# A diagonal LSTM and a quantum convolution on one core: the order of work inside the scan's ramp steps

## The chip, the core and the metric

The kernel runs on one core of a Trainium2 chip. The metric is the device time of one execution in microseconds, smaller is better. The core has five engines that run side by side, each working through its own queue in order: PE multiplies matrices (PEld is its loading of the weights, which can overlap a running product), DVE and ACT do element-wise work, POOL does element-wise work too and issues DMAs, SP issues DMAs. An engine waits for another by a semaphore.

## The reference

The input x has 16 images, 128 channels and 64 x 64 pixels. Layer 0 adds to x a diagonal LSTM of the group-normalised x; layer 1 adds a 1x1 quantum convolution of the result's group norm. The change touches layer 0 only:

```python
xs = skew(x)                                   # row i shifted right by i
i_s = einsum('oi,bihw->bohw', w_is, xs) + b_is
def step(carry, ist):
    h, c = carry
    h_shift = pad(h, ((0, 0), (0, 0), (1, 0)))[:, :, :-1]   # the row above
    s_s = einsum('oi,bih->boh', w_ss[:, :, 0], h_shift) + einsum('oi,bih->boh', w_ss[:, :, 1], h) + b_ss[None, :, None]
    gates = ist + s_s
    ofi = sigmoid(gates[:, :3 * C])
    o, f, ig = ofi[:, :C], ofi[:, C:2 * C], ofi[:, 2 * C:]
    g = tanh(gates[:, 3 * C:])
    c_new = f * c + ig * g
    h_new = o * tanh(c_new)
    return (h_new, c_new), h_new
_, hs = lax.scan(step, (h0, c0), i_s_t)
x = x + unskew(moveaxis(hs, 0, 3), W)
# layer 1: x + post_w @ simulate(pre_w @ group_norm(x))
```

A step of the scan works on one anti-diagonal. A row that the skewed picture has not reached sees zero input, so its state is the same for all images until its first pixel comes.

## The kernel before

It runs in three stages: the first group norm's statistics while x is loaded; the scan; then the second group norm and layer 1, which read and write DRAM. The work inside the scan is written under a manual schedule, so each engine's order is the order of the lines.

**Tiling of the scan.** Channels lie on the 128 partitions. The 64 rows are taken as two bands of 32 slots; band 1 starts BAND = 65 steps after band 0, and a slot that band 0 has left is taken by the row of band 1, so there are NSTEP = 160 steps, t = 0 to 159. Even slots are half q = 0 and odd slots half q = 1 of every tile, [128, 2, 256]; a column is one image of one slot, 16 (NB) to a slot. `columns(t)` gives the active columns a to b: they widen from 16 to 256 in steps 0 to 31, stay at 256 up to step 129, and shrink afterwards. `reach(t)` adds four columns past b, in which one column carries the state of the row that still waits for its first pixel.

**Two kinds of step.** A step whose half is at most FEW = 96 columns wide (`plain(t)`: steps 0 to 11 and 148 to 159) multiplies both halves of h by w1T and, shifted by a row, by w0T, for each gate (L768 to L771). The other 136 steps use that the row above an odd slot is the even slot of the same column: they multiply the even half of h by wsT = w0T + w1T into half 0 of all four gates (L774 to L775), ACT copies that half out (L789 to L792), and then each gate gets w1T times the difference of the two halves of h in half 1 and w0T times the difference towards the slot above in half 0 (L795 to L798). DVE adds the copy to half 1 (`add`, L757 to L760). `differences` (L602 to L610) makes the first difference on DVE (L604), the second on POOL (L607, L610). The gates go in the order ORDER = GF, GI, GG, GO (forget, input, candidate, output).

**The end of a step.** ACT applies the gate functions (`activate`, L762 to L766); DVE multiplies c by F (L806), then I by G (L812), adds it to c by halves (L815), ACT takes the tanh by halves (L816), and DVE multiplies by O into the next h by halves (L825). `gate_ps(t + 1)` (L578 to L593) puts the input products of the next step (L585) on PE meanwhile.

**New rows.** When a slot becomes active, `begin` (L599 to L600) spreads its one-column state over the 16 images: h from hinv on DVE, c from cinv on ACT (L829 to L831), in every step t with t + 1 < 32 for band 0, and with 64 <= t <= 95 for band 1. `waits` (L713 to L734) makes the next waiting state: its inner function `state` (L720 to L721) multiplies one column on DVE, once or twice, and POOL copies it into hinv and cinv.

**POOL and DVE beside it.** POOL subtracts the mean and scales by rstd for step t + 2 (`normalised`, L557 to L576), adds h to x in the ring (`residual`, L612 to L619), and keeps the last slot of band 0 as the edge for band 1 (L842 to L843). DVE takes the second norm's statistics as rows are finished (`statistics`). Four more operations on POOL prepare for the second norm: three memsets and one scaling, L642 to L645, which stand ahead of the scan.

Of the kernel before, what the change touches and what calls it, by code (L numbers as in the profile page):

```python
# [11 lines left out]
F32 = mybir.dt.float32  # L12
# [4 lines left out]
P = 128  # L17
NB = 16
NH = 64
NW = 64  # L20
SLOTS = 32
PAIRS = SLOTS // 2
NC = PAIRS * NB
RING = 40
ROWS = 4
BLOCK = ROWS * NW
# [2 lines left out]
FIRST = 8  # L29
LATE = 4  # L30
FEW = 96
LEAST = 128
AHEAD = RING - SLOTS
BAND = NW + 1
# [6 lines left out]
GO, GF, GI, GG = 0, 1, 2, 3  # L41
FUNC = {GO: AF.Sigmoid, GF: AF.Sigmoid, GI: AF.Sigmoid, GG: AF.Tanh}
ORDER = (GF, GI, GG, GO)
# [37 lines left out]
def kernel(  # L81
# [16 lines left out]
    nc = tc.nc  # L98
# [16 lines left out]
    group = wide_sb[:, 0:128]  # L115
# [7 lines left out]
    NG2 = NH // 4  # L123
# [32 lines left out]
    with ExitStack() as scan:  # L156
# [4 lines left out]
        wsT = wpool.tile([P, 512], F32, name="wsT")  # L161
        bias = wpool.tile([P, 4], F32, name="bias")

        hinv = wpool.tile([P, NH], F32, name="hinv")
        cinv = wpool.tile([P, NH], F32, name="cinv")
        state = scan.enter_context(tc.tile_pool(name="state", bufs=1))
# [50 lines left out]
        with ExitStack() as prep:  # L217
# [139 lines left out]
            for i in range(2):  # L357
                v = ws_n[i]
# [64 lines left out]
            ps = ps_small.tile([P, NB], F32, name="gv1", tag="small")  # L423
# [75 lines left out]
        work = scan.enter_context(tc.tile_pool(name="work", bufs=1))  # L499
        cst = work.tile([P, 2, NC], F32, name="cst")  # L500
# [10 lines left out]
        def columns(t):  # L511
            lo, hi = active(t)
            return lo // 2 * NB, (hi + 1) // 2 * NB
# [6 lines left out]
        def plain(t):  # L520
            a, b = columns(t)
            return b - a <= FEW

        def wide(t, least=LEAST):

            a, b = columns(t)[0], reach(t)
            return max(0, min(a, b - least)), max(b, min(NC, a + least))
# [50 lines left out]
        def gate_ps(t):  # L578

            a, b = wide(t, LEAST // 2)  # L580
            ps = {} if t else first
# [17 lines left out]
        def begin(copy, v, s, of, r):  # L599
            copy(one_slot(v, s), of[:, r : r + 1].to_broadcast([P, NB]))  # L600
# [37 lines left out]
        added = work.tile([P, 2, NB, 2], F32, name="added")  # L638
        inner = work.tile([P, NB, 2], F32, name="inner")
        sums_of = work.tile([P, 2, 2, NB], F32, name="sums_of")  # L640
        by_one = work.tile([P, P], F32, name="by_one")
        for v in (added, inner, sums_of):  # L642
            nc.gpsimd.memset(v, 0.0)
        by_half = group
        nc.gpsimd.tensor_scalar_mul(by_one, group, 1.0 / (NG2 * BLOCK))  # L645

        def early_sums():
            k = 2 * FIRST
# [64 lines left out]
        def waits(t, v, th, o, new):  # L713


            j = EARLY + t + 1
            to = columns(t + 1)[1]
            q = 1 if plain(t) else 0

            def state(at):  # L720
                nc.vector.tensor_mul(at, th[:, q, v : v + 1], o[:, q, v : v + 1])  # L721

            if to < NC:
                for k in range(q + 1):
                    if k != q or to > v:
                        state(new[:, k, to : to + 1])
                nc.gpsimd.tensor_copy(hinv[:, j : j + 1], new[:, q, to : to + 1])
            else:
                state(hinv[:, j : j + 1])
            nc.gpsimd.tensor_copy(cinv[:, j : j + 1], cst[:, q, v : v + 1])  # L730
            if to < NC:
                q1 = 1 if plain(t + 1) else 0
                if to > v or q1 != q:
                    nc.gpsimd.tensor_copy(cst[:, q1, to : to + 1], cinv[:, j : j + 1])  # L734

        def step(t, ps):

            a, b = columns(t)
            few = plain(t)
            a0, b0 = wide(t, LEAST // 2 if few else LEAST)  # L740
            w = reach(t)
            now, new, diff = hst[t % 2], hst[(t + 1) % 2], dst[t % 2]

            def product(g, out, w, rhs):
                nc.tensor.matmul(  # L745
                    out,
                    lhsT=w[:, g * 128 : (g + 1) * 128],
                    rhs=rhs,
                    start=False,
                    stop=True,  # L750
                    skip_group_check=True,
                )

            def half(g, q, w, rhs):
                product(g, ps[g][:, q, a0:b0], w, rhs[:, a0:b0])

            def add(g):  # L757
                if g in both:
                    v = ps[g][:, 1, a:b]
                    nc.vector.tensor_add(v, v, both[g][:, a:b])  # L760

            def activate(g):  # L762
                to = act[GG] if g == GG else ps[g]
                nc.scalar.activation(  # L764
                    to[:, :, a:w], ps[g][:, :, a:w], FUNC[g], bias=bias[:, g : g + 1]
                )  # L766

            if few and t:  # L768
                for g in ORDER:
                    product(g, ps[g][:, :, a0:b0], w1T, now[:, :, a0:b0])  # L770
                    product(g, ps[g][:, :, a0:b0], w0T, above(now, a0, b0))  # L771
            elif t:
                differences(t, now, diff)
                for g in ORDER:  # L774
                    half(g, 0, wsT, now[:, 0])  # L775
            if t > SLOTS:
                for _ in range(3):
                    next(steps, None)
            ready, sums[:] = list(sums), []
            statistics(4 if w - a <= LEAST else 6)  # L780
            if t:
                residual(t - 1, now)
            if t + 2 < NSTEP:
                normalised(t + 2)
            for later in ready:
                if next(later, True) is None:
                    sums.append(later)
            both = {}
            if not few:  # L789
                for g in ORDER:  # L790
                    both[g] = work.tile([P, NC], F32, name=f"both{t}_{g}", tag=f"both{g}")
                    nc.scalar.copy(both[g][:, a:b], ps[g][:, 0, a:b])  # L792
            act = {g: ps[g] for g in ORDER}
            act[GG] = work.tile([P, 2, NC], F32, name=f"g{t}", tag="g")
            if not few:  # L795
                for g in ORDER:
                    half(g, 1, w1T, diff[:, 1])
                    half(g, 0, w0T, diff[:, 0])  # L798
            add(GF)
            activate(GF)  # L800
            add(GI)
            activate(GI)
            add(GG)
            activate(GG)
            c = cst[:, :, a:w]
            nc.vector.tensor_mul(c, c, act[GF][:, :, a:w])  # L806
            add(GO)
            activate(GO)
            later = gate_ps(t + 1) if t + 1 < NSTEP else None

            ig = act[GI][:, :, a:w]
            nc.vector.tensor_mul(ig, ig, act[GG][:, :, a:w])  # L812
            th = act[GG]
            for q in range(2):
                nc.vector.tensor_add(c[:, q], c[:, q], ig[:, q])  # L815
                nc.scalar.activation(th[:, q, a:w], c[:, q], AF.Tanh)  # L816
            fresh = [
                (s, SLOTS * band + s)
                for band in range(2)
                for s in [t + 1 - BAND * band]  # L820
                if 0 <= s < SLOTS
            ]
            for q in range(2):
                v = w if q == few and columns(t + 1)[1] == b else b
                nc.vector.tensor_mul(new[:, q, a:v], th[:, q, a:v], act[GO][:, q, a:v])  # L825
                if q == few and w > b:
                    waits(t, b, th, act[GO], new)
                for s, r in fresh:
                    if s % 2 == q:  # L829
                        begin(nc.vector.tensor_copy, new, s, hinv, r)  # L830
                        begin(nc.scalar.copy, cst, s, cinv, r)  # L831
            if t == 1:
                nc.vector.memset(cst[:, :, LEAST:NC], 0.0)
            if t in (2, 3):
                nc.vector.memset(dst[t % 2], 0.0)
            if t >= NSTEP - LATE:
                by_scalar(NG2 - 2, NB - NSTEP + t)
            if t == NSTEP - 8:

                for n in range(4):  # L840
                    low_rows(nc.sync, n, spare[n])
            if SLOTS - 1 <= t < SLOTS - 1 + NW:  # L842
                nc.gpsimd.tensor_copy(edge[t - SLOTS + 1], one_slot(new, SLOTS - 1))  # L843
            return later
# [8 lines left out]
        with tc.manual_schedule():  # L853
            normalised(0)
            normalised(1)
            ps = gate_ps(0)
            for t in range(NSTEP):
                ps = step(t, ps)
# [4 lines left out]
            g, n = NG2 - 1, NB - LATE  # L863
# [5 lines left out]
            ps = ps_small.tile([P, 2, NB], F32, name="gm3", tag="small")  # L869
# [42 lines left out]
            ps = ps_small.tile([P, NB], F32, name="mr_ps", tag="small")  # L912
# [179 lines left out]
```

## Time and profile before

| what | value |
|---|---|
| median of 3 runs | 1429.56 us (1428.55 to 1434.26) |
| the profiled execution | 1429.22 us, of which its span 1427.4 us |
| mean granted clock of PE | 0.996 |
| L745 PE, the products of h: wsT, w1T, w0T | 241.4, 305.5, 305.5 us |
| L585 PE, the input's products | 481.3 us |
| L825 DVE, h: busy, idle before | 107.8 us, 45.2 us |
| L816 ACT, tanh of c: busy, idle before | 103.0 us, 64.3 us |
| L610 POOL, the difference to the slot above | 103.1 us, mean 758 ns |

The first row group of the page's costliest instructions is L585; the values are busy time, and the idle time is that of the engine just before the instructions of the group. A timeline line reads: start, busy time, engine, line, operation, output and inputs with shapes, number of instructions joined in it, and in brackets how long the engine had been idle and what released it. The page's slices of the span show three parts: loading, up to 103 us; the scan, from there to 1284 us; and the second norm with layer 1, in which the DMA engines are up to 99% busy.

### The profile page before, as it was taken

How to read it: one execution, taken by the hardware profiler on the slowest of the kernel's cores; microseconds unless marked ns; L12 is line 12 of the kernel's file. 1: busy time of each engine (PE TensorE's matmuls, PEld its weight loads, DVE VectorE, ACT ScalarE, POOL GpSimd, SP SyncE). 2: the span in 40 equal slices, each digit the busy share in tenths (PEclk: the TensorE clock that was granted, in tenths of full speed). 3: DMA queues.
4: the chain of work that ended last, by engine and by line, in shares of the span. 5: the costliest groups of instructions: out<-in, count | busy, mean ns of one | idle time of the engine just before them, and what ended most of it. 6: DMA issues, size and time to landing. Idle time of an engine off the chain costs nothing. (4 is left out here: it accounts for less than half of the span.)

```text
span 1427.4 us, 20012 instructions
## 1 busy us (share of the span) xinstructions
PE 1368.5 (96%) x5984; PEld 967.6 (68%) x5984; DVE 973.7 (68%) x2438; ACT 785.3 (55%) x1888; POOL 903.7 (63%) x1747
## 2 busy tenths in 40 slices
PE   6778999999999999999999999999999999988898
PEld 5658887777766777667667777766777777883232
DVE  7984566566665666887777776555555578777877
ACT  4555666555555555555555555555555566555231
POOL 3225777777766677788878877766666667642120
PEclk9999999999999999999999999999999999999999
DMA  9970000000000000133333100000000000106999
GB/s 325 369 275 1 1 1 1 1 0 1 1 0 1 1 0 1 60 118 119 118 118 118 60 1 1 1 1 0 1 1 1 1 1 1 31 2 217 359 365 326
DMA packets 87756, 107.05 MB, mean 75 GB/s; under 512 B 5424, under 2 KB 72016, under 8 KB 87648
## 3 DMA queue, kind: packets, MB, share of 16 engines
q1 hardware_dynamic: 82688, 93.34, 19.1%
q0 software_dynamic: 3728, 11.62, 2.5%
q8 instruction: 48, 0.79, 0.2%
q10 hardware_dynamic: 1232, 0.80, 0.2%
q14 instruction: 60, 0.49, 0.1%
HBM read 59.61 MB, written 46.14 MB: 74 GB/s over the span
## 5 line engine op out<-in xcount | busy, mean ns | idle before, releaser
L585 PE MATMUL ps<-xn,wxT 128*128 128x512 f32 (+18 forms) x1280 | 481.3, 519 | 1.7 <-POOL xn L576 1.7
L760 DVE TENSOR_TENSOR ps<-ps,both 128x256 f32<-128x256 f32 (+9 forms) x544 | 221.1, 408 | 315.4 <-PE ps L745 306.2
L764 ACT ACTIVATE ps<-ps,bias 128x512 f32<-128x512 f32 (+23 forms) x480 | 279.2, 583 | 220.8 <-DVE ps L760 184.6
L585 PEld LDWEIGHTS ps<-xn,wxT 128*128 128x128 f32 x1280 | 232.5, 192 | 174.2 <-issue 155.5
L745 PE MATMUL ps<-spare,w1T 128*128 128x256 f32 (+14 forms) x1088 | 305.5, 362 | 0.0
L745 PE MATMUL ps<-spare,w0T 128*128 128x256 f32 (+14 forms) x1088 | 305.5, 362 | 0.0
L792 ACT COPY both<-ps 128x256 f32<-128x256 f32 (+9 forms) x544 | 191.6, 355 | 178.3 <-PE ps L745 158.8
L619 POOL TENSOR_TENSOR ring<-ring,hst 128x256 f32<-128x256 f32 (+8 forms) x488 | 247.9, 540 | 21.0 <-DVE hst L825 21.0
L745 PEld LDWEIGHTS ps<-hst,wsT 128*128 128x128 f32 x1088 | 195.8, 190 | 85.6 <-DVE hst L825 36.7
L745 PE MATMUL ps<-hst,wsT 128*128 128x256 f32 (+14 forms) x1088 | 241.4, 365 | 5.4 <-DVE hst L825 4.1
L745 PEld LDWEIGHTS ps<-spare,w0T 128*128 128x128 f32 x1088 | 201.1, 190 | 21.2
L745 PEld LDWEIGHTS ps<-spare,w1T 128*128 128x128 f32 x1088 | 201.0, 190 | 21.1
L576 POOL TENSOR_TENSOR xn<-xn,rstd 128x512 f32<-128x512 f32 (+10 forms) x160 | 170.8, 1067 | 12.5
L571 POOL TENSOR_TENSOR xn<-ring 128x256 f32<-128x256 f32 (+8 forms) x213 | 147.0, 700 | 0.0
L825 DVE TENSOR_TENSOR hst<-g,ps 128x256 f32<-128x256 f32 (+13 forms) x320 | 107.8, 368 | 45.2 <-ACT g L816 42.7
L816 ACT ACTIVATE g<-cst 128x256 f32<-128x256 f32 (+20 forms) x320 | 103.0, 368 | 64.3 <-DVE cst L815 63.5
L566 POOL TENSOR_TENSOR xn<-ring,mean 128x16 f32<-128x16 f32 (+8 forms) x247 | 130.9, 540 | 7.5 <-DVE mean L143 6.1
L610 POOL TENSOR_TENSOR spare<-hst 128x240 f32<-128x240 f32 (+9 forms) x136 | 103.1, 758 | 35.5 <-DVE hst L825 31.6
L764 ACT ACTIVATE g<-ps,bias 128x512 f32<-128x512 f32 (+20 forms) x160 | 97.3, 608 | 28.4 <-DVE ps L760 22.2
L843 POOL COPY spare<-hst 128x16 f32<-128x16 f32 x64 | 25.1, 392 | 134.2 <-DVE hst L825 134.2
L815 DVE TENSOR_TENSOR cst<-cst,ps 128x256 f32<-128x256 f32 (+20 forms) x320 | 104.4, 368 | 5.5
L812 DVE TENSOR_TENSOR ps<-ps,g 128x512 f32<-128x512 f32 (+20 forms) x160 | 95.1, 594 | 17.7 <-ACT g L764 17.3
(355 smaller groups left out, 1244.0 us busy)
## 6 DMA issues: line engine op xcount, KB each, us to landing
ring<-in_x_dram SPq DMA_DIRECT2D x80, 256.0 KB, 5.6
out_dram<-ring SPq DMA_DIRECT2D x80, 256.0 KB, 5.0
low<-ring SPq DMA_DIRECT2D x6, 2048.0 KB, 7.8
ring<-in_x_dram SPq DMA_DIRECT2D x6, 2048.0 KB, 8.0
low<-low POOLq DMA_DIRECT2D x32, 256.0 KB, 5.6
out_dram<-low SPq DMA_DIRECT2D x32, 256.0 KB, 5.0
spare<-in_x_dram SPq DMA_DIRECT2D x27, 256.0 KB, 5.5
rest<-in_x_dram SPq DMA_DIRECT2D x21, 256.0 KB, 5.6
```

Of the source, the lines that this page charges most:

```text
L566: nc.gpsimd.tensor_sub(by_pairs(xn, 0, j, n), x0, over(mean1, n))
L571: nc.gpsimd.tensor_sub(by_pairs(xn, 1, j, n), lower, of)
L576: nc.gpsimd.tensor_mul(v, v, r)
L585: nc.tensor.matmul(ps[g][:, :, a:b], lhsT=wxT[:, g * 128 : (g + 1) * 128], rhs=xns[t % 2][:, :, a:b], start=t > 0, stop=True, skip_group_c ...
L610: nc.gpsimd.tensor_sub(diff[:, 0, a1:b], now[:, 1, a1 - NB : b - NB], now[:, 0, a1:b])
L619: nc.gpsimd.tensor_add(x1, x1, by_pairs(new, q, j, n))
L745: nc.tensor.matmul(out, lhsT=w[:, g * 128 : (g + 1) * 128], rhs=rhs, start=False, stop=True, skip_group_check=True,)
L760: nc.vector.tensor_add(v, v, both[g][:, a:b])
L764: nc.scalar.activation(to[:, :, a:w], ps[g][:, :, a:w], FUNC[g], bias=bias[:, g : g + 1])
L792: nc.scalar.copy(both[g][:, a:b], ps[g][:, 0, a:b])
L815: nc.vector.tensor_add(c[:, q], c[:, q], ig[:, q])
L825: nc.vector.tensor_mul(new[:, q, a:v], th[:, q, a:v], act[GO][:, q, a:v])
```

## The change

The diff does six things. The four preparing operations of POOL go into a function `prepared`, called at the end of step 32. The h state of a new row of band 0 is copied by POOL, after the differences and ahead of the residual, and the multiplication of half 1 stops ahead of that slot in even steps. `state` writes one or two columns with one operation, and in plain steps the multiplication no longer reaches past b. In all steps that are not plain, O's wsT product and its copy on ACT come behind F's w1T and w0T products. In steps where the half is over 96 and at most 176 columns wide (`short`: 12 to 21 and 138 to 147), G's tanh, the product of I and G, and O's sigmoid run by halves. The first states of band 1's rows come behind both multiplications of h.

```diff
--- before.py
+++ after.py
@@ -29,6 +29,7 @@
 FIRST = 8
 LATE = 4
 FEW = 96
+SHORT = 176
 LEAST = 128
 AHEAD = RING - SLOTS
 BAND = NW + 1
@@ -521,6 +522,11 @@
             a, b = columns(t)
             return b - a <= FEW
 
+        def short(t):
+
+            a, b = columns(t)
+            return FEW < b - a <= SHORT
+
         def wide(t, least=LEAST):
 
             a, b = columns(t)[0], reach(t)
@@ -639,10 +645,12 @@
         inner = work.tile([P, NB, 2], F32, name="inner")
         sums_of = work.tile([P, 2, 2, NB], F32, name="sums_of")
         by_one = work.tile([P, P], F32, name="by_one")
-        for v in (added, inner, sums_of):
-            nc.gpsimd.memset(v, 0.0)
         by_half = group
-        nc.gpsimd.tensor_scalar_mul(by_one, group, 1.0 / (NG2 * BLOCK))
+
+        def prepared():
+            for v in (added, inner, sums_of):
+                nc.gpsimd.memset(v, 0.0)
+            nc.gpsimd.tensor_scalar_mul(by_one, group, 1.0 / (NG2 * BLOCK))
 
         def early_sums():
             k = 2 * FIRST
@@ -718,15 +726,16 @@
             q = 1 if plain(t) else 0
 
             def state(at):
-                nc.vector.tensor_mul(at, th[:, q, v : v + 1], o[:, q, v : v + 1])
+                n = at.shape[1]
+                x, y = (u[:, q : q + 1, v : v + 1].to_broadcast([P, n, 1]) for u in (th, o))
+                nc.vector.tensor_mul(at, x, y)
 
             if to < NC:
-                for k in range(q + 1):
-                    if k != q or to > v:
-                        state(new[:, k, to : to + 1])
+                if q or to > v:
+                    state(new[:, 0 : q + 1, to : to + 1])
                 nc.gpsimd.tensor_copy(hinv[:, j : j + 1], new[:, q, to : to + 1])
             else:
-                state(hinv[:, j : j + 1])
+                state(hinv[:, j : j + 1].unsqueeze(1))
             nc.gpsimd.tensor_copy(cinv[:, j : j + 1], cst[:, q, v : v + 1])
             if to < NC:
                 q1 = 1 if plain(t + 1) else 0
@@ -759,10 +768,10 @@
                     v = ps[g][:, 1, a:b]
                     nc.vector.tensor_add(v, v, both[g][:, a:b])
 
-            def activate(g):
+            def activate(g, q=slice(0, 2)):
                 to = act[GG] if g == GG else ps[g]
                 nc.scalar.activation(
-                    to[:, :, a:w], ps[g][:, :, a:w], FUNC[g], bias=bias[:, g : g + 1]
+                    to[:, q, a:w], ps[g][:, q, a:w], FUNC[g], bias=bias[:, g : g + 1]
                 )
 
             if few and t:
@@ -771,11 +780,14 @@
                     product(g, ps[g][:, :, a0:b0], w0T, above(now, a0, b0))
             elif t:
                 differences(t, now, diff)
-                for g in ORDER:
+                for g in ORDER[:3]:
                     half(g, 0, wsT, now[:, 0])
             if t > SLOTS:
                 for _ in range(3):
                     next(steps, None)
+            if t + 1 < SLOTS:
+
+                begin(nc.gpsimd.tensor_copy, new, t + 1, hinv, t + 1)
             ready, sums[:] = list(sums), []
             statistics(4 if w - a <= LEAST else 6)
             if t:
@@ -786,51 +798,66 @@
                 if next(later, True) is None:
                     sums.append(later)
             both = {}
-            if not few:
-                for g in ORDER:
-                    both[g] = work.tile([P, NC], F32, name=f"both{t}_{g}", tag=f"both{g}")
-                    nc.scalar.copy(both[g][:, a:b], ps[g][:, 0, a:b])
+
+            def copy(g):
+                both[g] = work.tile([P, NC], F32, name=f"both{t}_{g}", tag=f"both{g}")
+                nc.scalar.copy(both[g][:, a:b], ps[g][:, 0, a:b])
+
             act = {g: ps[g] for g in ORDER}
             act[GG] = work.tile([P, 2, NC], F32, name=f"g{t}", tag="g")
             if not few:
+                for g in ORDER[:3]:
+                    copy(g)
                 for g in ORDER:
                     half(g, 1, w1T, diff[:, 1])
                     half(g, 0, w0T, diff[:, 0])
+                    if g == GF:
+                        half(GO, 0, wsT, now[:, 0])
+                        copy(GO)
             add(GF)
             activate(GF)
             add(GI)
             activate(GI)
             add(GG)
-            activate(GG)
+            parts_of = (slice(0, 1), slice(1, 2)) if short(t) else (slice(0, 2),)
+            for q in parts_of:
+                activate(GG, q)
             c = cst[:, :, a:w]
             nc.vector.tensor_mul(c, c, act[GF][:, :, a:w])
             add(GO)
-            activate(GO)
+            if not short(t):
+                activate(GO)
             later = gate_ps(t + 1) if t + 1 < NSTEP else None
 
             ig = act[GI][:, :, a:w]
-            nc.vector.tensor_mul(ig, ig, act[GG][:, :, a:w])
             th = act[GG]
+            if not short(t):
+                nc.vector.tensor_mul(ig, ig, th[:, :, a:w])
             for q in range(2):
+                if short(t):
+                    nc.vector.tensor_mul(ig[:, q], ig[:, q], th[:, q, a:w])
+                    activate(GO, slice(q, q + 1))
                 nc.vector.tensor_add(c[:, q], c[:, q], ig[:, q])
                 nc.scalar.activation(th[:, q, a:w], c[:, q], AF.Tanh)
-            fresh = [
-                (s, SLOTS * band + s)
-                for band in range(2)
-                for s in [t + 1 - BAND * band]
-                if 0 <= s < SLOTS
-            ]
             for q in range(2):
-                v = w if q == few and columns(t + 1)[1] == b else b
-                nc.vector.tensor_mul(new[:, q, a:v], th[:, q, a:v], act[GO][:, q, a:v])
+                v = w if q == few == 0 and columns(t + 1)[1] == b else b
+                if q == 1 and t + 1 < SLOTS and t % 2 == 0:
+                    v = b - NB
+                if a < v:
+                    nc.vector.tensor_mul(new[:, q, a:v], th[:, q, a:v], act[GO][:, q, a:v])
                 if q == few and w > b:
                     waits(t, b, th, act[GO], new)
-                for s, r in fresh:
-                    if s % 2 == q:
-                        begin(nc.vector.tensor_copy, new, s, hinv, r)
-                        begin(nc.scalar.copy, cst, s, cinv, r)
+            s = t + 1
+            if s < SLOTS:
+                begin(nc.scalar.copy, cst, s, cinv, s)
+            s -= BAND
+            if 0 <= s < SLOTS:
+                begin(nc.vector.tensor_copy, new, s, hinv, SLOTS + s)
+                begin(nc.scalar.copy, cst, s, cinv, SLOTS + s)
             if t == 1:
                 nc.vector.memset(cst[:, :, LEAST:NC], 0.0)
+            if t == SLOTS:
+                prepared()
             if t in (2, 3):
                 nc.vector.memset(dst[t % 2], 0.0)
             if t >= NSTEP - LATE:
```

## The prediction

> **What bounds the kernel now.** I read the page's busy table and its slices first, then busy time by stretch of time, then the timeline of one step of each kind.
>
> ```profile
> PE 1368.5 (96%) x5984; PEld 967.6 (68%) x5984; DVE 973.7 (68%) x2438; ACT 785.3 (55%) x1888; POOL 903.7 (63%) x1747
> PE   6778999999999999999999999999999999988898
> ...
> 100.00:140.00 40.00, 33.39 (x235) 30.46 (x236) 16.45 (x93) 19.19 (x68) 22.20 (x93) 0.96 0.01 1
> 140.00:200.00 60.00, 58.08 (x346) 49.49 (x345) 35.62 (x136) 38.65 (x117) 45.35 (x125) 1.00 0.01 1
> 300.00:400.00 100.00, 100.00 (x376) 71.11 (x375) 66.58 (x162) 56.06 (x117) 70.56 (x95) 1.00 0.00 1
> ...
> 1230.00:1260.00 30.00, 26.73 (x182) 24.77 (x181) 23.13 (x82) 16.37 (x50) 18.43 (x55) 1.00 0.12 36
> ```
>
> The columns of the last four are the stretch, its length, busy PE, PEld, DVE, ACT and POOL, the granted clock, DMA share and GB/s. In the steady steps (300 to 400) PE has no gap; the step from one first tanh to the next is 8.61 us there. In the ramps PE pauses every step: 6.6 of 40 us up to 140 us, 1.9 of 60 up to 200, 3.3 of 30 on the way down. Only in these pauses, and in the seam ahead of the first step, can the change gain; in the steady steps it can only cost. The first 103 us and the last 143 are outside what the diff touches.
>
> **What the Trainium skill says.** "Perfetto Trace Analysis", Optimizing Scalar/DVE Operations: "If Scalar/Vector aren't saturated, but are causing bubbles on other engines, breaking up instructions may allow work to be completed sooner." The ramps fit: neither engine is above 77% there, and PE waits for them. The same section gives each operation an overhead by engine and memory, and the trace shows what that does to halves: ACT's L764 on 256 columns takes 0.45 us, its L816 on 128 columns about 0.3, so half an operation costs two thirds of a whole. "SBUF — State Buffer", Who interferes with whom: a VectorE instruction with two SBUF inputs contends with a GpSimd one that reads SBUF. The trace agrees in direction: POOL's L610 on 128 columns took 0.56 to 0.65 us beside DVE's L604, 0.42 to 0.52 alone. I use it as a doubt about the copies that go to Pool.
>
> **Part 1, clearings out of the seam.**
>
> ```profile
> 103.79 0.15 POOL L643 MEMSET added<- 128x64 f32 x1 [2.34 <-DVE rstd L153]
> ...
> 104.76 0.25 POOL L576 TENSOR_TENSOR xn<-xn,rstd 128x32 f32<-128x32 f32 x1
> ...
> 105.07 3.68 PE L585 MATMUL ps<-xn,wxT 128*128 128x128 f32 x16 [1.67 <-POOL xn L576]
> ```
>
> Three memsets and the scaling stand on POOL between rstd and the multiply that PE's first product waits for. Without them the multiply starts where the first memset did: 104.76 - 103.79 = 0.97 us earlier, and the whole scan with it. What is next late is POOL's start states of c, which end about 0.17 us before the first c*f would need them; so all 0.97 counts. At step 32, where the four go, POOL has about 2.5 us to spare: cost nothing; uncovered, it would be about 1 us once. **-0.97** (0.7 to 1.0).
>
> **Part 2, the new rows' first states.** Up to step 30 each step has one copy of 16 columns on DVE (L600) less, one on POOL more. In the plain steps 0 to 11 the copy sits on the tail that PE waits for:
>
> ```profile
> 140.92 0.24 DVE L825 TENSOR_TENSOR hst<-g,ps 128x80 f32<-128x80 f32 x1 [0.25 <-ACT g L816]
> ...
> 141.07 0.17 DVE L600 COPY hst<-hinv 128x16 f32<-128x16 f32 x1
> 141.15 0.23 DVE L825 TENSOR_TENSOR hst<-g,ps 128x80 f32<-128x80 f32 x1
> 141.30 0.21 DVE L721 TENSOR_TENSOR hst<-g,ps 128x1 f32<-128x1 f32 x2
> 141.57 0.60 PE L745 MATMUL ps<-hst,w1T 128*128 128x200 f32 x2 [0.21 <-DVE hst L721]
> ```
>
> Step 9, odd: multiply, copy, multiply, two single-column states, then PE. Starts on DVE follow each other 0.08 (copy to multiply) and 0.15 apart, so the copy costs the tail 0.08, and joining the two states into one two-element operation takes one slot of some 0.03: -0.11. In even steps the copy is the last thing (it ends at 146.13 in step 10, the state at about 145.96): -0.17. Six of each: 6 x 0.17 + 6 x 0.11 = **-1.7** (1.0 to 2.3). POOL issues its copies (0.2 us each) after the differences and ahead of the residual, with about 1 us of slack a step or more: nothing; without the slack, up to 30 x 0.2 = 6 us.
>
> **Part 3, halves in the middle widths** (steps 12 to 21 and 138 to 147; GG's tanh, the product with I and O's sigmoid by halves). Step 144:
>
> ```profile
> 1225.34 0.48 ACT L764 ACTIVATE g<-ps,bias 128x256 f32<-128x256 f32 x1
> ...
> 1225.85 0.43 DVE L812 TENSOR_TENSOR ps<-ps,g 128x256 f32<-128x256 f32 x1
> ...
> 1226.31 0.48 DVE L815 TENSOR_TENSOR cst<-cst,ps 128x128 f32<-128x128 f32 x2
> ...
> 1226.69 0.51 ACT L816 ACTIVATE g<-cst 128x128 f32<-128x128 f32 x2 [0.38 <-DVE cst L815]
> ...
> 1227.11 0.49 DVE L825 TENSOR_TENSOR hst<-g,ps 128x128 f32<-128x128 f32 x2 [0.31 <-ACT g L816]
> 1227.45 1.16 PE L745 MATMUL ps<-hst,wsT 128*128 128x128 f32 x8 [0.37 <-DVE hst L825]
> ```
>
> GG, the product, c, tanh and h follow each other, and PE starts on h's first half. By halves that first half comes about 0.2 us sooner (0.1 from GG, 0.1 from the product). The second does not: the product of half 1 waits for c of half 0, so DVE runs product, c, product, c, and ACT has O's second sigmoid ahead of the second tanh; h's second half comes about 0.2 later, or 0.07 later in odd steps of the way up where the 16-column copy ahead of it is gone. DVE's difference of the two halves (L604, 0.29 us at 1227.62 here), which the w1T products need, then ends where it did. Ahead of those products PE now has three wsT products in place of four (part 4), three times 0.22 us at 128 columns: it starts 0.2 earlier, has 0.22 less to do, and waits. So I take 0.04 for the five even steps up and 0.14 for the odd: 5 x 0.04 + 5 x 0.14 = **-0.9** (-2.5 to +0.5), and for the way down, where no copy goes, **0** (-2.5 to +1.5). What PE loses in these steps beyond its own work, summed from the steps' periods, is 4.2 us up and some 6.3 down: no gain can be larger.
>
> **Part 4, O's wsT product and ACT copy behind F's products**, in all 136 steps that are not plain. PE's work is unchanged; w1T and w0T of F come one product earlier, 0.43 us in the steady steps, and need the differences of DVE and POOL that much earlier.
>
> ```profile
> 301.28 0.69 POOL L610 TENSOR_TENSOR spare<-hst 128x240 f32<-128x240 f32 x1
> ...
> 303.04 0.59 PE L745 MATMUL ps<-spare,w0T 128*128 128x256 f32 x2
> ```
>
> POOL's difference ends at 301.97, and PE's w0T is at 303.04; 0.43 earlier leaves 0.63. Over the steps this is 0.63 in steps 31 to 64, 0.43 or 0.70 in 65 to 95 (where POOL has an edge copy), 0.96 after; the smallest three are 0.19, 0.19 and 0.26 us. DVE's difference has 0.8 or more. No wait: **0**. F's gate being ready earlier gains nothing, since the step's end hangs on GG.
>
> **Part 5, the second band's first states behind both multiplies**, where the 16 even steps 64 to 94 had them between:
>
> ```profile
> 567.35 0.17 DVE L600 COPY hst<-hinv 128x16 f32<-128x16 f32 x1
> ...
> 567.58 1.15 PEld L745 LDWEIGHTS ps<-hst,wsT 128*128 128x128 f32 x5 [0.35 <-DVE hst L600]
> 567.89 1.03 PE L745 MATMUL ps<-hst,wsT 128*128 128x256 f32 x4
> ```
>
> The copy now ends about 0.21 later; the weight load follows at 567.79, and PE wants it at 567.89. That is 0 to 0.11 a step, 0 to 1.8 in all, 3.4 if none of the load hides: **+0.2**. The odd steps lose nothing.
>
> **Sum.** -0.97 - 1.7 - 0.9 + 0 + 0 + 0.2 = -3.4 us. The profiled execution took 1429.22 us (span 1427.4, 1.8 around it), 0.3 below the median of the runs, 1429.56; so 1429.22 - 3.4 = **1425.8**, with its own terms 1423 to 1429. About 0.5%, 7.15 us, is what a measurement of this kernel can tell from no change: faster is below 1422.4, slower above 1436.7.
>
> **The rivals.**
> A, the forecast: 0.52.
> B, halves pay in full. If the difference is not what PE waits for next, each of the 20 middle steps gains h's 0.2 and the 0.05 of the saved slot, with 0.75 more for copies in odd steps: 20 x 0.25 + 0.75 = 5.75 in place of 0.9, so -0.97 - 1.7 - 5.75 + 0.2 = -8.2, about 1421.0. For it: the measured wait is on h's first half. Against: the instruction order on DVE, and three products of cover. Chance 0.25.
> C, the lost cover decides, and the kernel is slower. It is one wait: F's w0T for POOL's difference. In the steps with an edge copy the margin is 0.43; POOL's time for the same operation varies by more than 0.1, and if its difference comes 0.6 us later than I read (its modelled ends are rough), each of 31 steps loses some 0.2: +6.2 - 3.4, about 1432. At 0.83 us late the steps 31 to 64 lose 0.2 too and these 31 lose 0.4: 31 x 0.4 + 34 x 0.2 - 3.4 = +15.8, about 1445. Against: even the smallest margin is above nothing. Chance 0.09, half of it beyond the slower mark.
> D, little arrives but the seam: the tails shortened in plain steps meet PE's own products, or the weight load eats them. -0.97 and the small +0.2: about 1428.4. For it: PEld is above 75% of those steps. Against: in step 9 PE waits on the state itself. Chance 0.14.
>
> **How the numbers follow.** The likeliest is A, 1425.8. The range is 1419.5 to 1432.0: below, B with half its uncertainty; above, D and the nearer part of C. Faster: most of B and the low edge of A, 0.24; slower: half of C, 0.05; within: 0.71.
>
> **What would show it.** Right: PE's first product about 1 us earlier; the tanh-to-tanh periods of steps 1 to 11 shorter by 0.1 to 0.2; those of steps 12 to 21 nearly so, 138 to 147 the same, with a new gap ahead of F's w1T; steady periods still 8.61; POOL's clearings at step 32 unnoticed. Wrong: idle PE ahead of w0T in steps 65 to 95 (C), or middle periods shorter by 0.2 or more (B).

## The result, and the profile after

The changed kernel took 1435.43 us (median of 11 runs, 1431.43 to 1437.43), the kernel before 1429.97 in its 11 runs (1427.63 to 1436.46). The ratio of the means (1434.85 and 1431.26) is 1.0025, with a 95% interval of 1.0009 to 1.0041: slower by 1.3 to 5.9 us, where 3.4 us faster was forecast. The median lies above the predicted range.

The profiled execution took 1437.43 us, 8.2 more than that of before. Not all of this is the change's: its statistics of the first norm were ready 1.68 us later, and from the last step's tanh to the end of the span it took 145.5 us in place of 142.9 (140.8 to 145.5 in all the kernels here, with the same code). Both stretches lie outside the diff, so from here on I compare the scan by its steps. The page's busy table, then busy time by stretch (the last stretch starts 3 us later than the one shown before, as the scan does there):

```profile
PE 1375.2 (96%) x5984; PEld 966.9 (67%) x5984; DVE 975.1 (68%) x2420; ACT 781.0 (54%) x1928; POOL 909.0 (63%) x1778
...
100.00:140.00 40.00, 34.26 (x238) 30.47 (x239) 16.94 (x81) 19.30 (x69) 22.85 (x99) 0.96 0.01 2
140.00:200.00 60.00, 57.55 (x338) 48.79 (x337) 34.87 (x126) 39.37 (x130) 46.28 (x135) 1.00 0.00 1
300.00:400.00 100.00, 100.00 (x370) 70.01 (x369) 68.24 (x165) 55.77 (x117) 68.85 (x93) 1.00 0.00 1
1233.00:1263.00 30.00, 26.75 (x181) 24.76 (x180) 23.04 (x82) 17.24 (x55) 18.65 (x55) 1.00 0.12 37
```

PE stays full in the steady steps. Between 140 and 200 us it pauses 2.45 us, 0.5 more than before, though the changed kernel is then in the same steps. The start of the first tanh of c in each step, read from the timeline, says where (us from one step's first tanh to another's; the last column is the whole scan, step 0 to 159):

| kernel | 0 to 11 | 11 to 23 | 30 to 130 | 137 to 149 | 0 to 159 |
|---|---|---|---|---|---|
| before | 42.08 | 68.86 | 862.10 | 64.13 | 1176.88 |
| changed | 41.13 | 71.86 | 862.52 | 66.17 | 1181.47 |
| e1_whole | 41.18 | 70.31 | 862.47 | 65.23 | 1178.88 |
| e2_four | 41.17 | 69.59 | 862.54 | 65.05 | 1178.13 |
| e3_dve | 41.17 | 72.22 | 862.53 | 66.20 | 1182.15 |
| e4_halves | 42.13 | 69.93 | 862.12 | 64.72 | 1178.42 |
| e5_rest | 41.12 | 68.83 | 862.44 | 64.14 | 1176.11 |
| e6_products | 41.14 | 70.75 | 862.52 | 65.67 | 1179.82 |
| e7_swap | 41.13 | 75.59 | 918.49 | 69.54 | 1252.06 |
| e8_pool | 41.13 | 70.65 | 862.51 | 65.67 | 1179.69 |
| e9_banks | 41.13 | 67.97 | 862.52 | 62.60 | 1173.96 |
| e10_banks_pool | 41.13 | 67.88 | 862.52 | 62.61 | 1173.86 |
| e11_between | 41.13 | 67.98 | 862.10 | 62.59 | 1173.54 |

The change gains 0.95 us in the plain steps and loses 3.00 on the way up in the middle widths, 2.04 on the way down and 0.42 in the steady stretch. With the rest (+0.08) the scan is 4.59 us longer. The seam gains 1.04, which leaves +3.55; the measured ratio of 1.0025 makes +3.6.

**The seam**, from the timeline of the changed kernel:

```profile
105.09 0.18 DVE L154 SCALAR_TENSOR_TENSOR rstd<-sq,r 128x16 f32<-128x16 f32 x1
105.41 0.25 POOL L582 TENSOR_TENSOR xn<-xn,rstd 128x32 f32<-128x32 f32 x1 [2.29 <-DVE rstd L154]
...
105.72 1.65 PE L591 MATMUL ps<-xn,wxT 128*128 128x128 f32 x6 [0.19 <-POOL xn L582]
```

PE's first product starts 0.45 us after the end of rstd (105.27); in the kernel before it started 1.48 us after it.

**A plain step**, step 8, even:

```profile
136.91 0.22 DVE L847 TENSOR_TENSOR hst<-g,ps 128x64 f32<-128x64 f32 x1 [0.19 <-ACT g L841]
137.05 0.15 DVE L731 TENSOR_TENSOR hst<-g,ps 128x2 f32<-128x2 f32 x1
...
137.31 0.30 PEld L754 LDWEIGHTS ps<-hst,w1T 128*128 128x128 f32 x2 [0.91 <-issue]
137.34 0.52 PE L754 MATMUL ps<-hst,w1T 128*128 128x168 f32 x2 [0.69 <-DVE hst L731]
```

The copy is gone from DVE, and h is complete at 137.20. But the weight load starts 0.12 us after that, where it started 0.05 us after the copy in the kernel before: it now waits for two engines, DVE and POOL.

**A middle step**, step 144, by the timeline (POOL's lines, O's first sigmoid and most of PE's are left out):

```profile
1229.51 0.63 ACT L773 ACTIVATE g<-ps,bias 128x128 f32<-128x128 f32 x2
...
1229.91 0.29 DVE L838 TENSOR_TENSOR ps<-ps,g 128x128 f32<-128x128 f32 x1
...
1230.24 0.29 DVE L840 TENSOR_TENSOR cst<-cst,ps 128x128 f32<-128x128 f32 x1
...
1230.62 0.31 ACT L841 ACTIVATE g<-cst 128x128 f32<-128x128 f32 x1 [0.24 <-DVE cst L840]
1230.63 0.30 DVE L838 TENSOR_TENSOR ps<-ps,g 128x128 f32<-128x128 f32 x1
...
1230.84 0.32 ACT L773 ACTIVATE ps<-ps,bias 128x128 f32<-128x128 f32 x1
1230.97 0.29 DVE L840 TENSOR_TENSOR cst<-cst,ps 128x128 f32<-128x128 f32 x1
...
1231.26 0.29 DVE L847 TENSOR_TENSOR hst<-g,ps 128x128 f32<-128x128 f32 x1
1231.29 0.31 ACT L841 ACTIVATE g<-cst 128x128 f32<-128x128 f32 x1
...
1231.61 0.94 PE L754 MATMUL ps<-hst,wsT 128*128 128x128 f32 x6 [0.36 <-DVE hst L847]
1231.70 0.29 DVE L847 TENSOR_TENSOR hst<-g,ps 128x128 f32<-128x128 f32 x1 [0.15 <-POOL inner L689]
1232.02 0.29 DVE L610 TENSOR_TENSOR spare<-hst 128x128 f32<-128x128 f32 x1
```

Count from the start of G's tanh. The first tanh of c comes at 1.11 (1.35 before), but h's first half at 1.75 (1.77 before). Two things stand ahead of it. c's second half has DVE from 1230.97 to 1231.26. And O's second sigmoid, which ACT runs between the two tanhs (1230.84), ends at 1231.16; it writes half 1 of the PSUM tile whose half 0 h's first half reads. h starts 0.10 us after that end, the distance that it kept from the end of the first tanh in the kernel before (1227.00 to 1227.11). The sigmoid is the later of the two: in step 143, where O's sigmoid is done long before, h's first half starts 0.08 us before c's second half ends, here 0.01 after it. h's second half comes at 2.19 (1.97 before), and the difference at 2.51 (2.28 before). So the 0.24 us at the first tanh were real, all but 0.02 of them were lost ahead of h's first half, and the second half came later.

**An even step on the way up**, step 16, has one more loss:

```profile
177.71 0.46 POOL L616 TENSOR_TENSOR spare<-hst 128x128 f32<-128x128 f32 x1
177.73 0.60 DVE L610 TENSOR_TENSOR spare<-hst 128x144 f32<-128x144 f32 x1
177.82 0.78 ACT L804 COPY both<-ps 128x144 f32<-128x144 f32 x3 [0.28 <-PE ps L754]
...
178.44 0.30 PEld L754 LDWEIGHTS ps<-spare,w1T 128*128 128x128 f32 x2 [0.38 <-ACT both L804]
```

The two differences read h at the same time. In the kernel before, DVE's began first and took 0.31; here POOL's began 0.02 us ahead, and DVE's took 0.60. This agrees with the Trainium skill, "SBUF — State Buffer", Who interferes with whom, for two operations that read SBUF: the page gives the two engines a read port in common, so below the one that starts second is said to lose the port. F's w1T is then loaded 0.12 us after DVE's difference ends (178.33). The bracket names ACT's copy, but the first of the three, F's, had ended at 178.10.

### The profile page after: what moved, and what is told of

Its sections match the earlier page's. It is cut to its first block, busy times and chain, and to the rows that moved or that the text cites. A ratio compares the mean times of both kernels' runs of the same rounds, so it can differ in the third digit from the quotient of the medians.

```text
span 1435.3 us, 20128 instructions
## 1 busy us (share of the span) xinstructions
PE 1375.2 (96%) x5984; PEld 966.9 (67%) x5984; DVE 975.1 (68%) x2420; ACT 781.0 (54%) x1928; POOL 909.0 (63%) x1778
## 5 line engine op out<-in xcount | busy, mean ns | idle before, releaser
L773 ACT ACTIVATE ps<-ps,bias 128x512 f32<-128x512 f32 (+26 forms) x500 | 284.7, 570 | 120.5 <-DVE ps L769 88.4
L754 PE MATMUL ps<-hst,wsT 128*128 128x256 f32 (+14 forms) x1088 | 263.4, 364 | 6.0 <-DVE hst L847 4.2
L847 DVE TENSOR_TENSOR hst<-g,ps 128x256 f32<-128x256 f32 (+17 forms) x319 | 107.0, 369 | 42.2 <-ACT g L841 37.8
L773 ACT ACTIVATE g<-ps,bias 128x512 f32<-128x512 f32 (+23 forms) x180 | 100.4, 569 | 25.8 <-DVE ps L769 19.7
L870 POOL COPY spare<-hst 128x16 f32<-128x16 f32 x64 | 21.1, 330 | 133.9 <-DVE hst L847 133.9
L826 DVE TENSOR_TENSOR cst<-cst,ps 128x512 f32<-128x512 f32 (+20 forms) x160 | 92.7, 579 | 15.3 <-POOL hst L606 10.8
```

Of the source, the lines that this page charges most:

```text
L754: nc.tensor.matmul(out, lhsT=w[:, g * 128 : (g + 1) * 128], rhs=rhs, start=False, stop=True, skip_group_check=True,)
L773: nc.scalar.activation(to[:, q, a:w], ps[g][:, q, a:w], FUNC[g], bias=bias[:, g : g + 1])
```

## The experiments

Three theories stood at first: the halves alone; O's later product alone; and three causes together (halves, the missing fourth product, and POOL's first states giving DVE's difference a second wait). Four kernels take one of these away, or add one. The expectations of these four count the way up from step 12, later ones and the table from step 11.

**e1_whole:** the halves out, the rest of the change in.

```diff
-SHORT = 176
+SHORT = FEW
```

> The changed kernel with the halves taken out: G's tanh, the product of I and G, and O's sigmoid run whole again in steps 12 to 21 and 138 to 147. I measure two stretches from the start of one first tanh of c to another: the way up, step 12 to step 23 (63.60 us before, 66.61 in the changed kernel), and the way down, step 137 to step 149 (64.13 and 66.17). Theory of three causes together (halves bring h's second half later by 0.1 to 0.2; one wsT product less stands ahead of F's w1T; the first states copied by POOL give DVE's difference a second wait, after which POOL takes the shared port first in even steps up): up about 65.6, since the port remains, down about 64.2, some 3 us faster than the changed kernel. Theory that the halves alone are the cause: 63.6 and 64.1, 5 us faster. Theory that O's later product alone is the cause: 66.6 and 66.2, no change.

Measured: up 64.85 in the stretch from step 12 (70.31 from step 11), down 65.23, ratio to before 1.0005 (0.9995 to 1.0015). None of the theories had this: without halves O's later product alone still costs 1.1 us down, where no first states exist and DVE's difference is as early as in the kernel before. The timeline of step 144 shows what PE waited for:

```profile
1227.99 0.29 DVE L610 TENSOR_TENSOR spare<-hst 128x128 f32<-128x128 f32 x1
...
1228.33 0.71 ACT L804 COPY both<-ps 128x128 f32<-128x128 f32 x3 [0.77 <-PE ps L754]
...
1228.65 0.30 PEld L754 LDWEIGHTS ps<-spare,w1T 128*128 128x128 f32 x2
1228.65 0.49 PE L754 MATMUL ps<-spare,w1T 128*128 128x128 f32 x2
```

DVE's difference ends at 1228.28. The first of ACT's three copies takes 0.27 and ends at 1228.60, and 0.05 later F's w1T loads: it writes half 1 of the PSUM tile whose half 0 the copy reads, and it is made to wait for the copy. With the load no longer ahead of time, its product is late by that load too. In every step from 13 to 22 and from 139 to 147 of this kernel the load starts 0.05 us after that copy. In the kernel before, it came 0.10 us after the copy here (1228.24 to 1228.33), so some 0.05 us of slack stood against the product of 0.22 that was moved away: 0.17 short, where this step lost 0.19. In the changed kernel the load starts 0.05 us after the copy in 12 of these 19 steps, and 0.12 after DVE's late difference in the other seven.

**e2_four:** O's wsT product and copy back ahead of F's products.

```diff
-                for g in ORDER[:3]:
+                for g in ORDER:
                     half(g, 0, wsT, now[:, 0])
...
-                    if g == GF:
-                        half(GO, 0, wsT, now[:, 0])
-                        copy(GO)
```

> The changed kernel with O's wsT product and its copy on ACT back ahead of F's products in all steps that are not plain; halves and POOL's first states stay. Same two stretches. Three causes together: the fourth product covers 0.22 to 0.28 us of the late difference, so up about 64.5 (even steps still lose some 0.2), down about 64.2; some 4 us faster than the changed kernel. Halves alone: 66.6 and 66.2, no change. O's later product alone: 63.6 and 64.1. The steady steps stay at 8.61 us in all three.

Measured: up 64.57, as the three causes said; down 65.05, 0.9 more than they said; ratio 1.0000 (0.9989 to 1.0010). So O's later product costs 3.3 us of the scan when the halves are there: 1181.47 in the changed kernel, 1178.13 here. Of the 0.9, 0.33 lies in step 143, where the second product of I and G starts that much late in this kernel and in the changed one, but not in e4_halves; it starts 0.04 us after the first tanh of c ends, on which it waits in no other middle step; why it does here is open. Another 0.24 lies at the end of step 147, in every kernel with the change's halves: step 148 is plain, so its first product reads both halves of h and waits for the late second one (2.43 us after G's tanh, 2.19 before).

**e3_dve:** band 0's first states back on DVE from step 12 on.

> The changed kernel with the first states of band 0 back on DVE, in the old place, in the steps that are not plain (12 to 30); in the plain steps POOL keeps them. Three causes together: DVE's difference has one wait again and takes about 0.31 us in place of 0.60 in the even steps, up about 65.4, down unchanged at 66.2. Halves alone, or O's later product alone: up 66.6 or more (the copies are back on DVE), down 66.2.

Measured: up 66.97, 0.35 longer than the changed kernel; down 66.20; ratio 1.0039 (1.0023 to 1.0056). The part of the theory on the second wait falls: in step 16 DVE's difference lost the port here too, since the copy stands ahead of it on DVE, and took 0.45, starting 0.16 after POOL's. What makes it late is h's second half: in e1_whole, with POOL's copies but h whole in time, DVE's difference of step 16 began 0.35 us ahead of POOL's.

**e4_halves:** the kernel before with the halves alone.

```diff
-            activate(GG)
+            for q in (slice(0, 1), slice(1, 2)) if short(t) else (slice(0, 2),):
+                activate(GG, q)
...
             for q in range(2):
+                if short(t):
+                    nc.vector.tensor_mul(ig[:, q], ig[:, q], th[:, q, a:w])
+                    activate(GO, slice(q, q + 1))
                 nc.vector.tensor_add(c[:, q], c[:, q], ig[:, q])
```

> The kernel before with the halves alone added, as in the changed kernel. Three causes together: no gain and little loss, since four wsT products cover the later second half: up 63.6 to 64.1, down 64.1 to 64.4. Halves alone as the cause: up 66.6, down 66.2. The reason for the halves (h's first half 0.2 us sooner): up and down each 1 to 2 us shorter.

Measured: up 64.89 from step 12 (69.93 from step 11, 1.07 longer than before), down 64.72, ratio 1.0022 (1.0012 to 1.0032). The halves lose by themselves, with four products of cover. On the way up, from G's tanh of step 16 to that of step 17 it is 0.20 us longer, from 17 to 18 0.01: the even steps pay, where the port is lost. On the way down 0.24 of the 0.59 is the end of step 147.

Alone, then, the halves cost 1.07 up and 0.59 down, and O's later product 1.45 and 1.10 (e1_whole against before; it has POOL's first states too, which e8_pool and e10_banks_pool find to be worth 0.1 us). Together they cost 3.00 and 2.04, 0.48 and 0.35 more than the sums. Up, the excess lies in the even steps 14 to 20, where DVE's late difference has one product less ahead of it. Down, 0.33 of it is step 143.

**e5_rest:** all three out; the clearings, the plain steps and band 1's order stay.

> The changed kernel without the halves, with O's wsT product and copy back ahead, and with band 0's first states on DVE in the steps that are not plain: what is left is the clearings, the plain steps and band 1's order. I now measure the way up from the first tanh of step 11 to that of step 23, since the halves bring the tanh of step 12 itself 0.2 us sooner (68.86 us before, 71.86 in the changed kernel, 70.31 without halves, 69.59 with the fourth product, 69.93 for halves alone). If halves and later product hold all of the loss: up 68.8 to 68.9, down 64.1, plain steps 0 to 12 some 0.9 us shorter than before; total 1 to 2 us faster than before. If something else of the change costs in these steps: up 69.3 or more.

Measured: up 68.83, down 64.14, ratio 0.9987 (0.9978 to 0.9996), 1.9 us faster than before. Both middle stretches are back at their old times, so nothing else of the change costs there.

**e7_swap** tests the copy: e1_whole with I's copy ahead of F's on ACT.

```diff
-                for g in ORDER[:3]:
+                for g in (GI, GF, GG):
                     copy(g)
```

> e1_whole (no halves, O's product later) with two of ACT's copies exchanged: I's copy before F's. Theory: with three wsT products ahead, F's w1T waits for ACT's copy of F's half 0 out of the same PSUM tile, which ends 0.05 us before the weight load; the copy now ends 0.25 us later, so each of the 20 middle steps loses about 0.25 us more: up 72.5 to 73, down 67.5 to 68. Theory that it waits for DVE's difference: 70.3 and 65.2, unchanged. In the steady steps 8.61 us either way, or slightly more if the copy is late there too.

Measured, one run: 1505.52 us; up 75.59, down 69.54, 5.28 and 4.31 more than e1_whole, and 0.56 more in each steady step. All three losses are larger than I wrote, but DVE's difference, which nothing changed, can't be the cause. They are larger because I's copy, now ahead, itself waits for I's wsT product: in step 144 F's copy starts 0.91 us after the first wsT product, in e1_whole 0.52. One wait of PE's weight loads, summed over this kernel (total in us, times, longest):

```profile
PEld ps L754 <- ACT both L804: 90.8, 136, 0.7
```

It occurs 136 times, once in each step that is not plain; the load starts 0.05 us after F's copy.

**e6_products** asks whether halves can pay: both products first, O's sigmoid whole, and the rest as in e5_rest.

```diff
+            for q in parts_of:
+                nc.vector.tensor_mul(ig[:, q], ig[:, q], th[:, q, a:w])
             for q in range(2):
-                if short(t):
-                    nc.vector.tensor_mul(ig[:, q], ig[:, q], th[:, q, a:w])
-                    activate(GO, slice(q, q + 1))
                 nc.vector.tensor_add(c[:, q], c[:, q], ig[:, q])
```

> As e5_rest, but with halves in another order: G's tanh by halves, both products of I and G by halves next, then c by halves; O's sigmoid whole, ahead of the tanh of c. My theory now: in the changed kernel DVE runs product, c, product, c, the second product waits for two engines, and h's first half stands behind c's second half on DVE, so that it gains nothing and the second comes 0.1 to 0.2 late. Here both halves of h come some 0.15 us sooner: up and down each 1 to 1.5 us shorter than e5_rest, and the kernel 4 to 5 us faster than before. If halves as such cost more in overheads than they save: up and down no shorter than e5_rest.

Measured: up 70.75, down 65.67, ratio 1.0018 (1.0010 to 1.0025): longer than e5_rest by 1.92 and 1.53, the wrong way. DVE in step 144:

```profile
1226.92 0.70 DVE L831 TENSOR_TENSOR ps<-ps,g 128x128 f32<-128x128 f32 x2
1227.66 0.48 DVE L833 TENSOR_TENSOR cst<-cst,ps 128x128 f32<-128x128 f32 x2
```

Two halves of c, in SBUF, overlap: 0.48 for two of 0.29. Two halves of the product, in one PSUM tile, do not: 0.70 for two of 0.3, with a pause of 0.10. The whole product took 0.43 in the kernel before.

**e8_pool:** as e6_products, first states on POOL throughout.

> As e6_products, but the first states of band 0 stay on POOL in all steps, which gives DVE's difference a second wait (POOL). If the second wait makes DVE start after POOL and lose the port in even steps (0.60 us in place of 0.31), up is 0.5 to 1 us longer than in e6_products; if h's second half is early enough, up is 0.5 us shorter, by the copies that DVE does not run. Down as e6_products.

Measured: up 70.65, down 65.67, ratio 1.0010 (0.9999 to 1.0020). Up is 0.1 us shorter, neither of the two expected ends. POOL's copies are neutral here.

**e9_banks:** as e6_products, each half's product in a PSUM tile of its own.

```diff
+                to = ps[GF][:, 0, a:w], ps[GG][:, 1, a:w]
+                for q in range(2):
+                    nc.vector.tensor_mul(to[q], ig[:, q], th[:, q, a:w])
...
-                nc.vector.tensor_add(c[:, q], c[:, q], ig[:, q])
+                nc.vector.tensor_add(c[:, q], c[:, q], to[q])
```

> As e6_products (both products of I and G first, O's sigmoid whole, four wsT products ahead, first states on DVE in steps 12 to 30), but each half's product is written to a PSUM tile of its own: half 0 into F's tile, half 1 into G's, both free by then. Theory: work on two halves of one PSUM tile is ordered by the whole tile, so that the second product waits for the first to end (0.10 us after it in e6_products), as F's w1T waits for the copy of the other half; with two tiles the second product starts 0.17 us sooner, c and both halves of h come some 0.13 us sooner than in the kernel before: up 67.3 to 67.8 (68.83 in e5_rest, 70.75 in e6_products), down 62.8 to 63.2 (64.14, 65.67), total 4 to 5 us faster than before. If halves cost by their number alone, whatever the tile: up 70.7, down 65.6.

Measured: up 67.97, down 62.60, ratio 0.9971 (0.9961 to 0.9981), 4.1 us faster than before. Down is a little better than written, up 0.2 short of it. Step 14 makes the difference: it is 0.16 longer than before, where the nine other middle steps on the way up are 0.05 to 0.14 shorter. Its first product starts 0.11 us after the second half of G's tanh, which it doesn't read; why is open. DVE in step 144:

```profile
1222.02 0.55 DVE L833 TENSOR_TENSOR ps<-ps,g 128x128 f32<-128x128 f32 x2
1222.48 0.47 DVE L838 TENSOR_TENSOR cst<-cst,ps 128x128 f32<-128x128 f32 x2
```

Only the tiles written have changed, and the two products now take 0.55 and c starts 0.46 after the first product in place of 0.74. The number of operations is that of e6_products, so it was not the overhead of halves that cost there.

**e10_banks_pool:** as e9_banks, first states on POOL throughout.

> As e9_banks with band 0's first states on POOL in all steps. e8_pool against e6_products was 0.1 us on the way up: DVE's difference started ahead of POOL's in both. So within 0.3 us of e9_banks on the way up, the same on the way down; if the second wait of DVE's difference gave POOL the port again, up is 0.5 us or more longer.

Measured: up 67.88, down 62.61, ratio 0.9976 (0.9962 to 0.9989): within 0.1 us of e9_banks by its steps. When h's second half is early, DVE's difference keeps its lead over POOL's (0.35 us in step 16).

**e11_between:** as e9_banks, band 1's first states between the multiplications again.

> As e9_banks with band 1's first states between the multiplications again, as in the kernel before. From the first tanh of step 30 to that of step 130 the two kernels with the old place take 862.10 and 862.12 us, the six with the new one 862.44 to 862.54. If the place is the cause: 862.1 here; if it is chance: 862.4 or more. All else as e9_banks.

Measured: 862.10 from step 30 to 130, ratio 0.9965 (0.9953 to 0.9977). All three kernels with the old place take 862.10 to 862.12, so the new place costs 0.42. It lies in two steps, 68 and 72, 0.21 each. This is the fastest of all by its steps, about 5 us below the kernel before by the ratio, though its interval and that of e9_banks overlap.

## Why the prediction was wrong, by its own steps

By parts, the change made -1.04 at the seam (part 1), -0.95 in the plain steps (part 2), +3.00 and +2.04 in the middle steps (parts 3 and 4), +0.42 in the steady ones (part 5) and +0.08 in the rest: +3.55.

**Part 1 (-0.97)** was right: 1.04 at the first product, and as much at the first tanh.

**Part 2 (-1.7)** had the right mechanism and little more than half the size. In step 8 the complete h comes 0.16 us sooner after the tanh, in step 9 0.125, as worked out, but PE's weight load, and with it the next tanh, only 0.10 and 0.06. The missing term is the second wait: POOL now writes part of h, so the load waits for two engines and starts 0.12 after DVE in place of 0.05. I priced POOL's copies by POOL's slack and did not ask what their reader waits for. Measured -0.95 from the tanh of step 0 to that of step 11. Nothing came at the end of step 11, which the sum counted too: step 12 is not plain.

**Part 3 (-0.9 up, 0 down)** failed at "By halves that first half comes about 0.2 us sooner". I noted that DVE runs product, c, product, c, and that ACT has O's second sigmoid ahead of the second tanh, and drew from both only that h's second half is late. h's first half stands behind c's second half on DVE and waits for that sigmoid, and gained 0.02. The statement that the difference "ends where it did" fell with it: 0.23 later in step 144, and in even steps up the port was lost besides. Nor did I see that the first product after step 147 needs h's second half. Cost by e4_halves: +1.07 and +0.59.

**Part 4 (0)** failed at "need the differences of DVE and POOL that much earlier": the margins in the steady steps held (no loss there), but the list of what F's w1T waits for was not complete. It waits for ACT's copy of F's other half, which itself starts only when F's wsT product is done. With 256 columns two more products cover the copy; with 128 columns, two products of 0.22 us do not cover a copy of 0.27 and the hand-overs before and after it. Cost by e1_whole: +1.45 and +1.10, and with the halves more.

**Part 5 (+0.2)** was right in sign and within its bounds of 0 to 1.8, but in part by luck: I spread a small loss over 16 even steps, and the +0.42 (e11_between) is two steps with the copy's whole slot, 68 and 72. PE idles 0.39 us ahead of the first wsT product at the end of step 68 in e11_between, 0.59 in e9_banks; in the other 14 steps nothing is lost.

**Rivals.** B, halves paying 0.25 us in each middle step, failed on those same two waits of h's first half; with O's sigmoid whole, both products first and the products in separate tiles (e9_banks) they pay 0.13 us from step 16's tanh of G to the next. C placed the lost cover in the steady steps, at POOL's difference. Lost cover did decide, but in the middle steps, at ACT's copy and DVE's difference. I had written the three products' wait into part 3 and let it cancel a gain that did not exist. D was right in part: the weight load ate some 0.06 us of each plain tail.

Not shown: why one step of a kernel, as step 143 here, has a wait that its neighbours don't, and what makes up the part of the halves' 0.59 on the way down that is not step 147. And no kernel kept the change's halves with only the order on DVE, or only O's sigmoid, altered, so these two waits of h's first half are read from the timeline and not told apart by a run.

## What to carry to other kernels

When a producer is moved ahead of its consumer's cover, list every semaphore of the consumer, not only the data it reads: here the waits that bit were for work on the other half of the same PSUM tile, ACT's copy for F's w1T and O's second sigmoid for h's first half. Before splitting an operation into halves, write down the engine's queue in the new order and ask what stands ahead of the half that was to be early and what the first reader of the other half is, and give halves that should overlap PSUM tiles of their own. A copy given to an idle engine isn't free if its reader then waits for two engines.

## What the runs showed of the hardware

Where an instruction waited for two engines or results in place of one, it started 0.06 to 0.07 us later: PE's weight load 0.12 after DVE in place of 0.05 (step 8), the second product 0.10 after the first in place of some 0.03 between dependent operations on DVE (e6_products). When DVE's and POOL's differences started close together, the one that came second took longer: DVE 0.60 in place of 0.31 us, 0.02 behind POOL (changed kernel, step 16), and POOL 0.58 in place of 0.46, 0.04 behind DVE (kernel before, step 16). Work on two halves of one PSUM tile ran one after the other, by DVE alone (e6_products) or across engines (F's w1T and ACT's copy in e1_whole and e7_swap); whether the tile or something smaller is the unit was not tested. The prediction's 0.56 to 0.65 and 0.42 to 0.52 us for POOL's L610 take in widths of 112 to 160 columns; on 128 it took 0.56 to 0.58 beside DVE's difference and 0.45 alone.
